# Pairwise products of fields: tile 0 of x in one transfer instead of four, and W issued after it

## The chip, the cores and the metric

The kernel runs on one core of one Trainium2 chip. The metric is the device time of one execution in microseconds (us). Before the change the median of four runs is 1289.72 us (1288.90 to 1290.04).

## The reference

`x` has 4096 samples of 32 fields with 64 values each, `W` is a 64 by 64 matrix, all in float32. Each field is multiplied by W, and then, for each of the 496 pairs of fields i < j, field i is multiplied element by element with the transformed field j.

```python
vid = jnp.einsum('bfd,de->bfe', x, W)
idx_i, idx_j = jnp.triu_indices(F_, k=1)
return x[:, idx_i, :] * vid[:, idx_j, :]
```

The output is 4096 x 496 x 64, some 520 MB, against 34 MB of input.

## The kernel before

**Tiles.** The batch is cut into 16 tiles of 256 samples. In a tile the 128 partitions hold 64 embedding values for each of two halves of the samples, and the free axis runs over 32 fields by 128 samples. A tile of x is thus 128 partitions by 4096 elements (2 MB), 16 KB in each partition. In HBM each partition's row of a tile has 8 fields of padding behind it.

**One large buffer.** `mem` (L122) holds everything in SBUF but W: places for tiles of x, given by `XPLACE`, and places for blocks of products, given by `SLOTS` as (number of pairs, place). The places overlap in time: a slot is written again after its transfer to HBM has ended. The first slots are 127 pairs at place 32, 126 pairs at place 159, and 63 pairs at place 32 again, so slot 2 needs the transfer of slot 0 to have ended.

**Work on a tile.** TensorE computes `vid` for a tile with 16 matmuls (L150): eight banks of four fields, two halves of the partitions each. In the profile each such matmul and its weight load count twice, so a tile has 32. `vid` fills all of PSUM and has one buffer, so the matmuls of the next tile wait for VectorE's reads of this one. VectorE writes the products into the slots with one `tensor_tensor` (L174) for each block that `by_block` and `products` lay out. The first block of a tile takes fields 0 to 15 alone, so VectorE's first product waits for the first half of the tile's matmuls. When a slot is full, SyncE issues its transfer to HBM (L177).

**Queues.** SyncE issues all transfers, in the order of the program, on one hardware queue served by 16 DMA engines. W goes first (L126), then tile 0 in four pieces of eight fields, then tiles 1 to 5 whole (all L135); 80 outputs (L177) and two further groups of five loads follow, the loads placed by `GROUPS`. A transfer that fills a place waits until what was there is no longer read.

The first matmul waits for W and for piece 1 of tile 0; the fifth, ninth and thirteenth wait for the other pieces.

Of the kernel before, what the change touches and what calls it, by code (L numbers as in the profile page):

```python
# [3 lines left out]

# [4 lines left out]

F32 = mybir.dt.float32  # L10
ALU = mybir.AluOpType

P = 128

C = 128

UNITS = 445

GROUPS = [6, 5, 5]
XPLACE = [285, 317, 349, 381, 413, 0, 285, 317, 349, 381, 413, 128, 96, 64, 32, 0]  # L20


SLOTS = [
    (127, 32), (126, 159), (63, 32), (64, 95), (84, 159), (63, 32),
    (74, 243), (84, 159), (95, 32), (71, 243), (116, 127), (95, 32),
    (106, 243), (116, 127), (95, 32), (106, 243), (116, 127), (95, 32),
    (127, 243), (116, 127), (95, 32), (127, 243), (116, 127), (43, 370),
    (95, 32), (95, 127), (63, 222), (95, 32), (84, 127), (74, 211),
    (84, 32), (95, 116), (74, 211), (116, 0), (95, 116), (74, 211),
    (116, 0), (95, 116), (105, 211), (105, 0), (105, 105), (105, 211),  # L30
    (105, 0), (105, 105), (127, 211), (105, 0), (105, 105), (127, 211),
    (105, 0), (106, 105), (56, 211), (95, 267), (51, 362), (107, 160),
    (73, 267), (73, 340), (84, 160), (84, 244), (95, 340), (84, 160),
    (95, 244), (105, 340), (84, 160), (96, 244), (105, 340), (105, 128),
    (106, 233), (105, 339), (127, 96), (116, 223), (106, 339), (127, 96),
    (116, 223), (106, 339), (127, 64), (127, 191), (127, 318), (127, 32),
    (127, 159), (120, 286),
]

XPAD = 8  # L40
OPAD = 24


STARTS = [0, *accumulate(n for n, _ in SLOTS)]


def by_block():


    def within(lo):  # L50
        yield "step", lo, 2, 1, 0
        for k in range(2):
            yield "step", lo, 4, 2, k
        for i in (lo, lo + 8):
            yield "row", i + 4, i, 4, 4
        yield "row", lo + 8, lo, 8, 8

    yield from within(0)
    yield "row", 16, 0, 16, 16
    yield from within(16)  # L60


def products(blocks, at=0):

    for kind, a, b, c, d in blocks:
        if kind == "row":
            rows, n, i0, di, j0, dj = c, d, b, 0, a, 1
        else:
            rows, n, i0, di, j0, dj = 16 // b, c, a, b, a + c + d, b
        r = k = 0  # L70
        while r < rows:
            room = STARTS[bisect_right(STARTS, at)] - at
            if k or room < n:
                m, w = 1, min(n - k, room)
            else:
                m, w = min(rows - r, room // n), n
            yield at, m, w, i0 + r * di + k, di, j0 + r * dj, dj
            at += m * w
            if k + w == n:
                r, k = r + m, 0  # L80
            else:
                k += w


def pairs(blocks):

    for _, m, w, i, di, j, dj in products(blocks):
        for r in range(m):
            for k in range(w):
                yield i + r * di + k, j + r * dj  # L90


@with_exitstack
def pairwise_bilinear_kernel(
    ctx: ExitStack,
    tc: tile.TileContext,
    x: bass.AP,
    w: bass.AP,
    out: bass.AP,
):  # L100

    nc = tc.nc
    NT = x.shape[0]
    F = x.shape[2] - XPAD
    D = P // 2
    NP = F * (F - 1) // 2

    BANK = 512 // C


    ctx.enter_context(tc.manual_schedule(engines={mybir.EngineType.SP}))

    const = ctx.enter_context(tc.tile_pool(name="const", bufs=1))
    psum = ctx.enter_context(
        tc.tile_pool(name="ps", bufs=1, space=bass.MemoryType.PSUM)
    )
    vid = psum.tile([P, F, C], F32)  # L120

    mem = const.tile([P, UNITS, C], F32)  # L122


    w2 = const.tile([P, D], F32)
    nc.sync.dma_start(out=w2, in_=w)  # L126

    loaded = []

    def load(pieces=1):  # L130
        t = len(loaded)
        xt = mem[:, XPLACE[t] : XPLACE[t] + F, :]
        n = F // pieces
        for lo in range(0, F, n):
            nc.sync.dma_start(out=xt[:, lo : lo + n, :], in_=x[t][:, lo : lo + n, :])  # L135
        loaded.append(xt)

    load(4)
    for _ in range(GROUPS[0] - 1):
        load()  # L140
    groups = iter(GROUPS[1:])

    for t in range(NT):
        xt = loaded[t]


        for b in range(0, F, BANK):
            for h in range(2):
                half = slice(h * D, (h + 1) * D)
                nc.tensor.matmul(  # L150
                    vid[half, b : b + BANK, :],
                    lhsT=w2[half, :],
                    rhs=xt[half, b : b + BANK, :],
                    start=True,
                    stop=True,
                )

        for at, m, w, i, di, j, dj in products(by_block(), t * NP):
            slot = bisect_right(STARTS, at) - 1
            n = m * w  # L160
            begin, end = STARTS[slot], STARTS[slot + 1]
            ot = mem[:, SLOTS[slot][1] : SLOTS[slot][1] + SLOTS[slot][0], :]
            o = ot[:, at - begin : at - begin + n, :]
            if m == 1:
                left = xt[:, i : i + w, :]
                right = vid[:, j : j + 1, :].to_broadcast([P, w, C])
            else:
                o = o.rearrange("p (m w) c -> p m w c", m=m)
                right = vid[:, j : j + (m - 1) * dj + 1 : dj, :].unsqueeze(2).to_broadcast([P, m, w, C])
                if di == 0:  # L170
                    left = xt[:, i : i + w, :].unsqueeze(1).to_broadcast([P, m, w, C])
                else:
                    left = xt.rearrange("p (m d) c -> p m d c", d=di)[:, i // di : i // di + m, i % di : i % di + w, :]
            nc.vector.tensor_tensor(o, left, right, ALU.mult)  # L174
            at += n
            if at == end:
                nc.sync.dma_start(out=out[:, begin:end, :], in_=ot)  # L177


        if t + 2 == len(loaded) < NT:  # L180
            for _ in range(next(groups)):
                load()


_INS = ["r_x", "L0_rec_W"]
_OUTS = [((4096, 496, 64), "float32")]


# [37 lines left out]
```

## Time and profile before

| | |
|---|---|
| median of 4 runs | 1289.72 us |
| the profiled execution, its time | 1289.47 us |
| its span, first to last instruction | 1287.7 us |
| VectorE busy | 1087.8 us, 407 instructions |
| TensorE busy, matmuls | 221.4 us, 512 records |
| moved by the DMA queue of SyncE | 553.69 MB |
| HBM read, written | 33.59 MB, 520.09 MB |

The page of the profile has busy times of each engine, the span in 40 slices, the DMA queues, the chain of work that ended last, and the costliest groups of instructions. The answers of the trace give instructions in order of time, the chain in a window, and busy times, DMA share and GB/s in any stretch. In a stretch's line the columns are: the stretch, its length, the busy times of TensorE's matmuls, its weight loads (PEld), VectorE (DVE) and GpSimd (POOL) with their counts, TensorE's granted clock, the share of the DMA engines, and the GB/s that started in it. A packet is booked at its start; in short stretches the share can so exceed 1. "SPq" is SyncE issuing a transfer.

### The profile page before, as it was taken

What the parts mean: (1) busy time and instruction counts of PE and PEld (TensorE: products, weight loads), DVE (VectorE), ACT (ScalarE), POOL (GpSimd) and SP (SyncE); (2) the same over time, 40 slices, a digit from 0 to 9 for tenths busy, and PEclk for the clock granted to TensorE, in tenths of its full rate; (3) what the DMA queues carried; (4) which work ended last, traced back from release to release, by engine and by line L of the source; (5) the groups of instructions that cost most, each with busy time, mean ns of one, the idle gap of its engine ahead of it and who ended that gap; (6) DMA issues with size and microseconds to landing.
All of it is one profiled execution on the core that took longest, in us unless ns stands there. A gap on an engine that the chain in (4) does not pass through costs nothing.

```text
span 1287.7 us, 1768 instructions
## 1 busy us (share of the span) xinstructions
PE 221.4 (17%) x512; PEld 41.0 (3%) x512; DVE 1087.8 (84%) x407; POOL 0.2 (0%) x4
## 2 busy tenths in 40 slices
PE   4031221312012013040313111103121121202000
PEld 1000000000000000000000000000000000000000
DVE  6799999998948399899999887369999998989960
POOL 0000000000000000000000000000000000000000
PEclk7555555556556555555555655555565565655555
DMA  9999999999999999999999999999999999999998
GB/s 386 455 414 443 426 430 448 433 436 432 424 435 415 427 435 428 441 431 436 428 443 434 427 438 423 429 428 436 430 437 437 432 433 437 433 435 433 430 442 359
DMA packets 14409, 553.79 MB, mean 430 GB/s; under 512 B 1728, under 2 KB 1728, under 8 KB 2240
## 3 DMA queue, kind: packets, MB, share of 16 engines
q1 hardware_dynamic: 14400, 553.69, 99.7%
q8 instruction: 4, 0.07, 0.0%
q14 instruction: 5, 0.04, 0.0%
HBM read 33.59 MB, written 520.09 MB: 430 GB/s over the span
## 4 chain that ended last, share of the span: by engine, by line
DMA 48%; DVE 45%; issue 3%; SPq 0%; PE 0%; another core or an unknown queue 0%; DVEq 0%
DMA out_dram<-mem 47%; DVE mem L174 45%; SPq L135 0%; PE vid L150 0%; DMA mem<-in_r_x_dram 0%; DVEq L214 0%; DVEq L174 0%; SPq L126 0%
## 5 line engine op out<-in xcount | busy, mean ns | idle before, releaser
L174 DVE TENSOR_TENSOR mem<-mem,vid 128x1024 f32<-128x1024 f32 (+16 forms) x407 | 1087.8, 2746 | 155.6 <-DMA out_dram<-mem 143.1
L150 PE MATMUL vid<-mem,w 64*64 64x512 f32 x512 | 221.4, 988 | 954.1 <-DVE mem L174 902.3
L150 PEld LDWEIGHTS vid<-mem,w 64*64 64x64 f32 x512 | 41.0, 196 | 1132.8 <-DVE mem L174 1061.5
L196 POOL MEMSET const-bfloat16-1.0<- 128x1 bf16 x1 | 0.1, 102 | 0.0
L196 POOL MEMSET const-uint8-127<- 128x1 uint8 x1 | 0.1, 102 | 0.0
L196 POOL MEMSET const-float32-0.0<- 128x1 f32 x1 | 0.1, 99 | 0.2 <-issue 0.2
L196 POOL MEMSET const-float32-1.0<- 128x1 f32 x1 | 0.1, 99 | 0.0
## 6 DMA issues: line engine op xcount, KB each, us to landing
out_dram<-mem SPq DMA_DIRECT2D x12, 8128.0 KB, 35.2
out_dram<-mem SPq DMA_DIRECT2D x13, 6720.0 KB, 32.9
out_dram<-mem SPq DMA_DIRECT2D x14, 6080.0 KB, 31.4
out_dram<-mem SPq DMA_DIRECT2D x9, 7424.0 KB, 31.6
out_dram<-mem SPq DMA_DIRECT2D x8, 5376.0 KB, 24.0
out_dram<-mem SPq DMA_DIRECT2D x6, 6784.0 KB, 34.7
mem<-in_r_x_dram SPq DMA_DIRECT2D x15, 2048.0 KB, 25.1
out_dram<-mem SPq DMA_DIRECT2D x4, 4736.0 KB, 26.7
```

The lines of the kernel that those rows point to most:

```text
L150: nc.tensor.matmul(vid[half, b : b + BANK, :], lhsT=w2[half, :], rhs=xt[half, b : b + BANK, :], start=True, stop=True,)
L174: nc.vector.tensor_tensor(o, left, right, ALU.mult)
L196: nc = _bacc.Bacc("TRN2", target_bir_lowering=False, num_devices=1, dynamic_dma_scratch_size=1024)
```

## The change

Tile 0 is loaded by one transfer of 128 x 4096 elements in place of four of 128 x 1024, and W's transfer (128 x 64) is issued after it. Tiles 1 to 5 follow W as before. The first matmul now waits for the whole of tile 0 and for W; no later matmul of tile 0 waits for a transfer. SyncE issues three transfers fewer. The order and shapes on TensorE and VectorE are as before.

```diff
     w2 = const.tile([P, D], F32)
-    nc.sync.dma_start(out=w2, in_=w)
 
     loaded = []
 
-    def load(pieces=1):
+    def load():
         t = len(loaded)
         xt = mem[:, XPLACE[t] : XPLACE[t] + F, :]
-        n = F // pieces
-        for lo in range(0, F, n):
-            nc.sync.dma_start(out=xt[:, lo : lo + n, :], in_=x[t][:, lo : lo + n, :])
+        nc.sync.dma_start(out=xt, in_=x[t][:, :F, :])
         loaded.append(xt)
 
-    load(4)
+    load()
+    nc.sync.dma_start(out=w2, in_=w)
     for _ in range(GROUPS[0] - 1):
         load()
```

## Prediction

> **What bounds the kernel now.** I read the 40 slices and the DMA queues of the page first, because a kernel that moves 554 MB is likely to be bound by that.
>
> ```profile
> DVE  6799999998948399899999887369999998989960
> ...
> DMA  9999999999999999999999999999999999999998
> ...
> q1 hardware_dynamic: 14400, 553.69, 99.7%
> ```
>
> The row to read is DMA: nine tenths or more in every slice, the first included. VectorE has slices of 3, 4 and 6 tenths, so it runs out of buffers and not out of time. One stretch from the view by stretches makes this sharper.
>
> ```profile
> 2.00:1283.00 1281.00, 221.38 (x512) 40.98 (x512) 1087.81 (x407) 0.00 (x0) 0.54 1.00 432
> ```
>
> The last two columns are the DMA share, 1.00, and GB/s, 432. From the first bytes to the last the 16 engines never stand still: time = first byte (about 2 us) + 553.69 MB at 432 GB/s + a tail. An edit can move the end only if it moves the first byte, changes what the bytes cost, or opens a hole in the stream. The list of waits agrees: VectorE's largest is 143.1 us in 34 waits for output transfers, so it is ahead of the stream and loses a delay at its next wait.
>
> The change lies in the first 35 us, so I next read the chain of waits there.
>
> ```profile
> 0.73 0.38 SPq L126
> 1.11 0.06 issue
> 1.17 4.05 DMA mem<-in_r_x_dram
> 5.21 0.14 issue
> 5.35 5.35 PE vid L150 x16
> 10.70 0.02 issue
> 10.73 34.48 DVE mem L174 x10
> ```
>
> W is issued at 0.73, piece 1 of tile 0 at 1.17, it lands at 5.21, TensorE starts 0.14 later and VectorE at 10.73. VectorE then runs through slots 0 and 1 without a gap. SyncE's timeline shows when slot 0 goes out, and the source view of that issue gives 24.8 us to landing:
>
> ```profile
> 28.23 0.35 SPq L177 DMA_DIRECT2D out_dram<-mem  x1
> ```
>
> **Is slot 0 late or early now?** The same two views give, for the last load (tile 5), issue at 5.46 and 28.4 us to landing: 33.86. Slot 0 lands at 28.23 + 24.8 = 53.03, which is 19.17 us after the loads; 8128 KB at 434 GB/s take just that. So slot 0 started only when the loads were through, and was issued about 5 us before its turn. The turn itself is in the narrow stretches:
>
> ```profile
> 32.00:32.50 0.50, 0.00 (x0) 0.00 (x0) 0.50 (x1) 0.00 (x0) 0.50 0.97 360
> 32.50:33.00 0.50, 0.00 (x0) 0.00 (x0) 0.50 (x1) 0.00 (x0) 0.50 2.42 1041
> ```
>
> A packet's bytes are booked at its start, and slot 0's packets (65 KB a partition) are the largest so far: the jump to 1041 GB/s is their start. The 16 engines turn to slot 0 between about 32.6 and 33.5; I call it 33.0. The cover from the issue at 28.23 is 4.8 us, from which the time between an issue and its first bytes has to be taken.
>
> **The change, part by part.**
>
> (a) *W no longer goes first.* Tile 0 is issued at 0.73 in W's place and not at 1.17: 0.44 us earlier. Bytes follow an issue by 1.0 us here: W, issued at 0.73, has its first in the stretch 1.70:1.80, and tile 0, issued at 1.17, its first in 2.20:2.30. Thus tile 0's bytes start near 1.8, and every load with them: -0.44 us for the stream.
>
> (b) *Four pieces become one transfer.* Three issues of about 0.43 us go from SyncE; SyncE is ahead of the stream anyway (the last load, issued at 5.46, lands at 33.86), so they are worth nothing. A partition's row becomes 16 KB in place of four of 4 KB. The pieces land 4.0, 4.9, 5.7 and 6.5 us after issues at 1.17, 1.64, 2.10 and 2.58, so at 5.2, 6.5, 7.8 and 9.1: about 1.29 us apart, 5.16 us for four. Whole tiles, landing at 13.95 (tile 1), 18.80, 23.73 and 28.65, are 4.9 us apart. Gain about 0.25 us; by rounding between 0.1 and 0.35.
>
> (c) *W sits behind tile 0.* Its 32 KB pass almost wholly between 1.70 and 2.10, before there is anything else to move. Now they stand in the full stream. The cost is between nothing and these 0.4 us; I take 0.2, since the bytes alone are below 0.1 us at 432 GB/s and the packets are small (256 B).
>
> The loads' end so moves by -0.44 - 0.25 + 0.2 = -0.5 us: slot 0's turn is 32.5 in place of 33.0.
>
> (d) *The first matmul waits for all of tile 0 and then W,* where it waited for a quarter of the tile. Tile 0 lands at 9.1 - 0.44 - 0.25 = 8.4, W 0.2 later at 8.6, and with the 0.14 us of before TensorE starts near 8.75 and not at 5.35: 3.4 us late. Queued behind that matmul on TensorE are the other 15 of tile 0; waiting for the first half of them is VectorE's first product, and for that SyncE's issue of slot 0.
>
> (e) *TensorE's first 5.35 us* set VectorE's start. Its weight loads show two paces:
>
> ```profile
> 7.08 0.27 PEld L150 LDWEIGHTS vid<-mem,w 64*64 64x64 f32 x2 [0.59 <-issue]
> 7.93 0.27 PEld L150 LDWEIGHTS vid<-mem,w 64*64 64x64 f32 x2 [0.59 <-issue]
> 8.79 0.16 PEld L150 LDWEIGHTS vid<-mem,w 64*64 64x64 f32 x2 [0.59 <-issue]
> 9.22 0.15 PEld L150 LDWEIGHTS vid<-mem,w 64*64 64x64 f32 x2 [0.28 <-issue]
> ```
>
> The steps are 0.86 us until 8.79, then 0.43, though the granted clock stands at 1.00 throughout. Piece 2 landed at 6.5 and is first needed at 7.93, so the pieces did not slow it. If the slow stretch goes with the start of work, it comes again and VectorE starts 3.4 us late, at 14.1. If it goes with the time since the program began, all eight steps are fast and 1.7 us come back; if nothing speeds up in time, four steps more are slow, +1.7. I take 3.4, the row as it stands. The Trainium skill ("TensorE: Matmul & The Clock Gate", section "What's actually happening") lets the clock rise after about 3.4 us of activity, in a window that runs freely: the 3.4 us from 5.35 to 8.79 agree, and by it the slow stretch returns with some scatter.
>
> (f) *Slot 0* is then issued at 28.23 + 3.4 = 31.6 in place of 28.23. Its bytes can start 1.0 us later by the rows in (a): 32.6. No row shows an output's own lead. The nearest hint is the stretch 30.50:31.00, the first in which the loads fall below 400 GB/s, 2.3 us after slot 0's issue: if that is its first effect, the bytes can start only at 33.9. Between 32.6 and 33.9 against a turn of 32.5 the hole is 0.1 to 1.4 us; I take 0.7.
>
> (g) *Behind slot 0* nothing is late. Slot 1 is issued 17.0 us behind slot 0 (45.22 now) and slot 0's transfer lasts 19.2 us. VectorE, which idles 7.94 us until slot 0's buffer is free, idles less instead. The hole passes on as it is; there is no spare time in a stream with a share of 1.00 to win it back.
>
> **Sum.** -0.5 (a to c) + 0.7 (f) = +0.2 us. The profiled execution took 1289.47 us, 1.8 more than its span of 1287.7, and that remainder is untouched. It lies 0.25 below the median of 1289.72, so as a median I say 1289.9. A difference of 0.2% (2.6 us) is about what a measurement of this kernel can tell from no change.
>
> A rule that speaks against the change: the Trainium skill, "Perfetto Trace Analysis", section "DMA Optimizations", says that splitting a transfer can let some of the work start sooner, if the DMA engines are generally idle. Here 3.4 us of TensorE's start go with the split, but the DMA share is 1.00, so the rule's condition fails. By the rule alone the end would be 3.4 us later; by the rows above, 0.2.
>
> **Rivals.**
>
> *A, the cover suffices.* The slow stretch of TensorE does not come again, or an output's lead is under 0.9 us. There is no hole, the stream keeps the gain of (a) to (c), and the time is 1289.7 - 0.5 = 1289.2. For it: slot 0's cover of 4.8 us. Against it: 3.4 + 1.0 use 4.4 of it, and the turn comes 0.5 sooner.
>
> *B, W is late and a hole opens: slower.* Its place is W's transfer, issued between tile 0 and tile 1. If its small packets do not pass in order but share the engines with tile 1, W lands with tile 1, near 13.95 - 0.5 = 13.4; TensorE starts at 13.6, 8.2 us late, slot 0 is issued at 36.4 and flows at 37.4, 4.9 us behind its turn: +4.4 us with the gain taken off, 1294.1. The change turns slower by over 2.6 us when slot 0 is issued after about 34.6 (32.5 + 0.5 + 2.6 - 1.0), that is when TensorE starts after 11.7. Against it: loads land strictly in the order of issue in this trace.
>
> *C, a longer cold start.* Slow steps all along (+1.7) and the long lead (2.3) add up: slot 0 flows at 28.23 + 5.1 + 2.3 = 35.6, 3.1 behind its turn, +2.6: 1292.3. It needs both at once.
>
> *D, the edit changes nothing.* The four pieces are one block in memory and in HBM, so they could have flowed as one all along. But the landings 1.29 us apart and TensorE's start at the first show that they count one by one.
>
> **How the numbers follow.** Forecast, a small hole about cancelled by the gain: 0.62, 1289.3 to 1291.0. A: 0.26, 1288.6 to 1289.4. C, whole or in part: 0.08. B: 0.04. The forecast, A but for 0.01 of it, and half of C lie within 0.2%: same 0.91. Slower 0.08 from B and the rest of C. Faster gets A's 0.01: nothing in (a) to (c) is worth 2.6 us. The range, 1288.7 to 1291.6, takes in the forecast, nearly all of A and the lower half of C.
>
> **What would show it.** In the profile after: tile 0's single landing near 8.4 and W's near 8.6; TensorE from 8.75; VectorE from 14.1; slot 0 issued at 31.6; a short hole or none near 32.5 to 33.5 in the narrow stretches; slot 0's landing within 1 us of 53.03. I would be wrong if W landed well past 9, if the DMA share fell anywhere later, or if VectorE's lateness were still to be seen after slot 2.

## The result, and the profile after

The changed kernel takes 1291.04 us (median of 42 runs, 1289.48 to 1292.11), the kernel before 1289.57 us (60 runs, 1288.81 to 1291.02). The ratio is 1.0011 with a 95% interval of 1.0007 to 1.0015: slower by 1.5 us. That lies within the forecast range of 1288.7 to 1291.6 and within 0.2%, but the likeliest case said +0.2 us, and the median lies just above the 1289.3 to 1291.0 that the forecast gave that case. So the question for the experiments is where the other 1.3 us come from. The profiled execution has a span of 1289.0 us where before had 1287.7.

The 40 slices and the long stretch of the changed kernel show almost nothing; this is what a change of 0.1% looks like in an average.

```profile
DMA  9999999999999999999999999999999999999998
...
2.00:1284.00 1282.00, 220.88 (x512) 41.11 (x512) 1087.91 (x407) 0.00 (x0) 0.55 1.00 432
```

The chain of waits of the changed kernel in the first 75 us answers to the one of before:

```profile
0.73 0.37 SPq L132
1.10 0.05 issue
1.15 7.75 DMA w<-in_L_rec_W_dram
8.90 0.14 issue
9.03 5.84 PE vid L148 x16
14.88 0.02 issue
14.90 34.48 DVE mem L172 x10
49.38 0.02 issue
49.40 22.70 DMA out_dram<-mem
```

W is now what TensorE waits for; it lands at 8.90. TensorE starts 3.7 us later than before, needs 5.84 us for the first half of tile 0 and not 5.35, and VectorE starts 4.2 us later. VectorE's 34.48 us are the same to the hundredth. Slot 0 is issued 17.5 us after VectorE's start, at 32.40:

```profile
32.40 0.35 SPq L175 DMA_DIRECT2D out_dram<-mem  x1
```

The narrow stretches of the changed kernel show the hole (DMA share and GB/s are the last two columns):

```profile
31.00:31.50 0.50, 0.07 (x2) 0.07 (x4) 0.50 (x2) 0.00 (x0) 0.50 1.15 492
31.50:32.00 0.50, 0.50 (x2) 0.22 (x4) 0.50 (x1) 0.00 (x0) 0.50 0.39 164
32.00:32.50 0.50, 0.50 (x4) 0.16 (x2) 0.50 (x2) 0.00 (x0) 0.50 0.08 33
32.50:33.00 0.50, 0.50 (x4) 0.07 (x2) 0.50 (x1) 0.00 (x0) 0.50 0.00 0
33.00:33.50 0.50, 0.50 (x4) 0.23 (x2) 0.50 (x1) 0.00 (x0) 0.50 4.88 2081
```

Before, there was no stretch without bytes between the loads and slot 0. Now the loads are through near 32, nothing starts between 32.5 and 33.0, and then all 16 engines begin their 65 KB packets within one half microsecond: 2081 GB/s is twice the 1041 and 1040 of the two stretches of before, since there the engines came to slot 0 one after another. The packet records of the trace give the same in finer steps. The first packets of slot 0 start between 32.72 and 33.53 us before, and between 33.25 and 33.40 after. The hole has set the engines **in step**.

### The profile page after: what moved, and what is told of

Same layout as the page of the kernel before. It is cut to its first block, busy times and chain, and to the rows that moved or that the text cites. A ratio compares the mean times of both kernels' runs of the same rounds, so it can differ in the third digit from the quotient of the medians.

```text
span 1289.0 us, 1764 instructions
## 1 busy us (share of the span) xinstructions
PE 220.9 (17%) x512; PEld 41.1 (3%) x512; DVE 1087.9 (84%) x407; POOL 0.2 (0%) x4
## 4 chain that ended last, share of the span: by engine, by line
DMA 51%; DVE 42%; issue 2%; SPq 0%; PE 0%; another core or an unknown queue 0%; DVEq 0%
DMA out_dram<-mem 50%; DVE mem L172 42%; DMA w<-in_L_rec_W_dram 1%; SPq L132 0%; PE vid L148 0%; DVEq L212 0%; DVEq L172 0%
```

## The experiments

Theory H: the cost is the hole before slot 0, and the hole comes from slot 0's readiness alone. Its rival R: the single transfer, or W's small packets in the full stream, cost in themselves. In the table, "flow" is the start of slot 0's first packets (of its first part where it is cut in two); "landing" is the end of the last packets of the whole of slot 0, averaged over the 16 engines (the prediction's 53.03 is the moment at which the last engine reported it, which is later); the medians have the kernel before on the same chip beside them.

| run | flow, us | landing, us | median, us | before, us | ratio (95% interval) |
|---|---|---|---|---|---|
| before | 32.7 to 33.5 | 52.21 | 1289.57 | | |
| the change | 33.25 to 33.40 | 52.57 | 1291.04 | 1289.57 | 1.0011 (1.0007 to 1.0015) |
| e1 whole tile, W first | 33.24 to 33.39 | 52.56 | 1291.28 | 1289.61 | 1.0012 (1.0004 to 1.0021) |
| e2 pieces, W second | 32.4 to 33.7 | 52.17 | 1289.29 | 1289.61 | 0.9999 (0.9990 to 1.0008) |
| e3 change, slot 0 in two | no hole | 52.25 | 1289.04 | 1289.61 | 0.9995 (0.9986 to 1.0004) |
| e4 W after tile 1 | 37.22 to 37.37 | 56.54 | 1295.86 | 1289.61 | 1.0047 (1.0034 to 1.0060) |
| e6 before, slot 0 in two | no hole | 52.36 | 1289.89 | 1289.33 | 1.0004 (0.9995 to 1.0013) |
| e7 pieces, W last | 33.70 to 33.85 | 53.02 | 1291.12 | 1289.33 | 1.0014 (1.0006 to 1.0023) |

**e1, the whole tile with W first.**

```diff
-    load(4)
+    load(1)
```

> One part of the change alone: tile 0 in one transfer, W still first. Theory H (the time is set by when slot 0 can flow; after the loads the stream stands still until then): tile 0 lands near 9.0, TensorE starts near 9.2, slot 0 is issued near 32.5 as in the changed kernel, so the hole is about as large and the time is 1290.8 to 1291.3, as with the whole change. Rival R (the cost is W's small packets inside the full stream, or W landing last): W lands at 2.5 again, so the time falls back to 1289.3 to 1289.7.

It took 1291.28 us, as H said: W is in place long before, and the time is that of the whole change.

**e2, four pieces with W behind the first.**

```diff
             nc.sync.dma_start(out=xt[:, lo : lo + n, :], in_=x[t][:, lo : lo + n, :])
+            if t == 0 and lo == 0:
+                nc.sync.dma_start(out=w2, in_=w)
```

(and W's first issue taken out)

> The gain of an early tile 0 without its cost: four pieces, W behind piece 1. H: piece 1 lands near 4.8 and W near 5.0, TensorE starts near 5.2, slot 0 is issued near 28.2, no hole; the stream starts 0.4 us earlier, so 1289.1 to 1289.6, at or just under the kernel before. R (W's packets in the full stream cost): 1290 or more.

1289.29 us. TensorE starts at 4.63, slot 0 is issued at 27.79, and there is no hole. W's small packets stand in the full stream here and do no harm; R falls on both its halves together with e1 and e7.

**e3, the changed kernel with slot 0 in two transfers.**

```diff
-    (127, 32), (126, 159), (63, 32),
+    (56, 32), (71, 88), (126, 159), (63, 32),
```

> The changed kernel with slot 0 cut in two transfers, 56 and 71 pairs, at the same places; no VectorE instruction changes. The first is ready near 23 us, well before the loads end. H: the hole is gone although TensorE still starts near 9.0, and the time falls to 1288.9 to 1289.6. R (the single transfer, or W's place in the stream, costs in itself): stays at 1291.0.

1289.04 us, 2.0 us under the changed kernel. The chain of this run shows that nothing was mended in front:

```profile
1.16 7.72 DMA w<-in_L_rec_W_dram
8.88 0.14 issue
9.01 6.06 PE vid L148 x16
15.07 0.02 issue
15.09 28.26 DVE mem L172 x9
```

TensorE and VectorE start as late as in the changed kernel. But the first part of slot 0 is issued at 23.00, the loads run into it without a gap, and the late start costs nothing. Against the kernel before the median is 0.57 us lower; the interval takes in no change.

**e6, the same cut in the kernel before.** The edit is that of e3.

> Control for the run with slot 0 in two: the same cut in the kernel before, where slot 0 is not late. H: nothing to win, 1289.3 to 1289.8. If the cut itself brought the gain: 1288.8 or less.

1289.89 us, just above the upper end: the cut itself wins nothing, and e3's gain is the hole's.

**e7, four pieces with W behind all of them.**

```diff
-    nc.sync.dma_start(out=w2, in_=w)
...
     load(4)
+    nc.sync.dma_start(out=w2, in_=w)
```

> The other part alone: tile 0 in four pieces, W behind all four. H: W lands near 9.0, TensorE starts near 9.1, slot 0 flows near 33.3 as in the changed kernel: a hole of the same kind and 1290.8 to 1291.4. R (the single transfer is what costs): 1289.3 to 1289.7.

1291.12 us. Either part of the change alone brings the whole cost (1.7 us in e1 and 1.8 in e7 over the kernel before, 1.5 for both together), and the two do not add up, since each only sets when TensorE has both W and data.

**e4, more of it: W behind tile 1 as well.**

```diff
     load()
+    load()
     nc.sync.dma_start(out=w2, in_=w)
-    for _ in range(GROUPS[0] - 1):
+    for _ in range(GROUPS[0] - 2):
```

> Dose: the changed kernel with W behind tile 1 as well, so W lands near 13.7, TensorE starts near 13.9 and slot 0 is issued near 37.2, 4.9 us later than in the changed kernel. H: the hole grows by as much and passes on one for one: 1295.4 to 1296.2. If VectorE's lead won some of it back, or the hole were not the cause, less: 1291 to 1293.

1295.86 us. In the narrow stretches the hole is plain; between 32.5 and 37.0 the engines stand still.

```profile
34.00:36.00 2.00, 0.60 (x2) 0.29 (x4) 2.00 (x2) 0.00 (x0) 0.50 0.00 0
36.00:37.00 1.00, 1.00 (x4) 0.23 (x2) 1.00 (x2) 0.00 (x0) 0.50 0.00 0
37.00:37.50 0.50, 0.50 (x4) 0.23 (x2) 0.50 (x1) 0.00 (x0) 0.50 4.87 2081
```

Slot 0 flows 3.97 us later than in the changed kernel, and the span of the profiled execution is 4.1 us longer (1293.1 against 1289.0). More hole passes on one for one between these two executions; e4's is the fastest of its five, and the medians are 4.8 us apart. The 4.9 us expected of slot 0's issue were 4.0, because TensorE's first half took 5.00 us in this execution.

**What is still open after these.** In the changed kernel slot 0 lands 0.36 us later than before (52.57 against 52.21), and the end is 1.5 us later. Something is lost behind slot 0. The stretches at work show where. First before, then the changed kernel:

```profile
54.00:140.00 86.00, 15.77 (x32) 2.33 (x32) 83.20 (x35) 0.00 (x0) 0.50 1.00 433
170.00:340.00 170.00, 31.40 (x72) 5.71 (x72) 160.11 (x56) 0.00 (x0) 0.55 1.00 434
```

```profile
54.00:140.00 86.00, 15.53 (x32) 2.33 (x32) 83.02 (x35) 0.00 (x0) 0.52 1.00 431
170.00:340.00 170.00, 30.93 (x72) 5.71 (x72) 159.25 (x56) 0.00 (x0) 0.56 1.00 433
```

The DMA share is 1.00 in all four, so no engine idles, yet the bytes move more slowly. In the packet records, bytes over duration give the rate of one engine while it works (large packets alone, so e5's own small writes are left out):

| GB/s per engine | 54 to 113 us | 170 to 340 us | 840 to 1280 us |
|---|---|---|---|
| before, e2, e3, e6 | 27.05 | 27.08 | 27.08 |
| the change, e1, e4, e7 | 26.94 | 27.02 | 27.08 |
| e5 (six writes) | 27.02 | 27.02 | 27.08 |
| e11 (one write) | 26.98 | 27.02 | 27.08 |

The two upper rows agree to 0.01 in every one of their kernels, so this is no scatter: kernels with a hole move their packets 0.4% and then 0.2% more slowly, until about the second group of loads, and not at all after it. From slot 0's landing to that of the output near 341 us the stream takes 288.22 us before and 289.15 after, averaged over the engines: 0.93 us. Theory L: engines that the hole has put in step slow one another. Rivals: the output rows' places in HBM collide when the engines are in step (P), or something else is late.

**e8, e9 and e10, other row distances in HBM** (the kernel changed, changed, and before).

```diff
-OPAD = 24
+OPAD = 26   # e8, e10
+OPAD = 32   # e9
```

> The changed kernel with the padding behind each output row in HBM at 26 units of 512 B in place of 24, so that rows of neighbouring partitions lie at other distances. If the packets between 54 and 340 us are slow behind the hole because engines in step write to rows that collide in HBM (theory P), their rate there moves away from 26.94 and 27.02 GB/s per engine, up or down by 0.1 or more. If it is the engines being in step as such (theory L), the rates stay within 0.02 of these, and the time near 1291.

> The same with 32 units. P: another rate again, by 0.1 or more off 26.94 and 27.02. L: both stay within 0.02, time near 1291.

> Control: the kernel before with 26 units, where the engines are spread over 0.8 us from the start. L: 27.05 and 27.08 GB/s per engine as before, 1289.3 to 1289.9. P: its rate moves too, by 0.05 or more.

e8 took 1290.96 us (ratio to before 1.0014, 1.0005 to 1.0024) with 26.94 and 27.02 GB/s per engine; e9 took 1290.85 (1.0014, 1.0004 to 1.0023) with 26.94 and 27.02; e10 took 1289.31 (1.0002, 0.9992 to 1.0011) with 27.05 and 27.08. No rate moves with these two distances: P falls for them.

**e5 and e11, the engines put out of step again.** Small writes right behind slot 0 keep some engines longer than others.

```diff
                 nc.sync.dma_start(out=out[:, begin:end, :], in_=ot)
+                if slot == 0:   # e5
+                    for p0, p1, u in (0, 14, 0), (0, 11, 7), (0, 9, 14), (16, 23, 0), (16, 21, 7), (16, 18, 14):
+                        nc.sync.dma_start(out=out[p0:p1, NT * NP + u : NT * NP + u + 7, :], in_=ot[p0:p1, u : u + 7, :])
...
+                if slot == 0:   # e11
+                    nc.sync.dma_start(out=out[0:8, NT * NP : NT * NP + 24, :], in_=ot[0:8, 0:24, :])
```

> The changed kernel with six small writes issued right behind slot 0, into the unused rows behind the output: 3.5 KB from each of 14, 11, 9, 7, 5 and 2 partitions, so that the DMA engines, which the hole has set to the same phase, are spread over about 0.8 us again. They cost 0.4 us averaged over the engines and 0.8 for the one hit most; the output is the reference's. Theory L (engines in step move packets more slowly): from slot 0's landing to the landing of the output issued before the second group of loads the stream takes 288.2 to 288.5 us averaged over the engines, as without a hole, in place of 289.15, and the packets between 54 and 113 us move at 27.04 GB/s per engine in place of 26.94; the time is 1290.4 to 1291.3, no worse than the changed kernel. Rival (the loss behind slot 0 comes from late fetches or waits, not from the engines' phase): 289.1 and 26.94 stay, and the writes come on top: 1291.4 to 1291.9.

> The changed kernel with one write right behind slot 0, 12 KB from each of 8 partitions into the unused rows behind the output, so that 8 of the 16 DMA engines fall about 0.46 us behind the other 8 (0.23 us averaged); the output is the reference's. Theory L (engines in step slow one another, whichever they are): with only 8 in step the loss is about halved, 26.99 GB/s per engine or more between 54 and 113 us and 27.05 between 170 and 340, and the time stays at 1290.7 to 1291.2. If the slowing is between engines that this write shifts together: 26.94 and 27.02 stay, and the write comes on top, 1291.2 to 1291.6. If it is between engines that it parts: 27.05 and 27.08 return, 1290.3 to 1290.7.

Both are misses in time: e5 took 1293.87 us (ratio to before 1.0031, 1.0020 to 1.0042), e11 1292.18 (1.0018, 1.0009 to 1.0027). The writes cost far more than I gave them: e11's 12 KB packets took 1.6 to 2.2 us each, where 0.46 was expected. The stretch from slot 0's landing to the output near 341 us, for which e5's expectation had 288.2 to 288.5 us under L and 289.1 under its rival, took 290.1; the writes' own cost is in it, so it decides nothing. In the packets right behind, L does show. Slot 1's 128 packets of 64,512 bytes last 2.380 us in all cases before, in 16 after the change (the others up to 2.41), in 101 in e5 and in 57 in e11. Parting the engines so brings back the flat duration, for a time. It does not last: between 170 and 340 us e5 and e11 are at 27.02 like the changed kernel, where L had 27.05 or more.

The starts of the packets say more. Near 298 us, in the changed kernel, 14 of the 16 engines still start within 0.22 us of one another. In e5 at the same place the 16 starts are spread over 2.08 us of a packet's 2.40, wider than the 1.74 of before, and the packets are as slow as the changed kernel's. So being in step cannot be the whole cause there. L is supported right behind slot 0, where the phase was set by hand; what slows the packets between 170 and 340 us stays open.

## Why the prediction was right, and where it was not

**(a) to (c), the gain of 0.5 us.** Right. Tile 0's first packet starts at 1.74 in place of 2.21. The times are too coarse for the three terms, but the landings, as the engines report them and averaged over the 16, tell them apart. The last piece of tile 0 landed at 8.56 before and at 8.10 in e7, where the pieces go first: 0.46 us for (a), forecast 0.44. Tile 0 in one transfer landed at 8.30 in e1, where W goes first as before: 0.26 for (b), forecast 0.25. Tile 1 followed tile 0 by 5.00 us in the changed kernel and 5.01 in e7, with W between them, and by 4.90 in e1 and 4.89 before: 0.1 for (c), forecast 0.2. That makes 0.6 us. The whole sum without a hole is e3: 0.57 us under before, though its interval takes in zero.

**(d) TensorE's start.** 9.03, forecast 8.75. Tile 0 landed at 8.7 and not 8.4: on average over the engines it landed at 7.8, but one of the 16 was half a microsecond behind the others, and TensorE waits for the last.

**(e) TensorE's two paces.** The slow steps came again, as taken, and five of them in place of four: 5.84 us. The first half's weight loads show the turn near 13.5:

```profile
11.62 0.26 PEld L148 LDWEIGHTS vid<-mem,w 64*64 64x64 f32 x2 [0.59 <-issue]
12.47 0.26 PEld L148 LDWEIGHTS vid<-mem,w 64*64 64x64 f32 x2 [0.59 <-issue]
13.33 0.22 PEld L148 LDWEIGHTS vid<-mem,w 64*64 64x64 f32 x2 [0.59 <-issue]
13.83 0.15 PEld L148 LDWEIGHTS vid<-mem,w 64*64 64x64 f32 x2 [0.28 <-issue]
14.26 0.15 PEld L148 LDWEIGHTS vid<-mem,w 64*64 64x64 f32 x2 [0.28 <-issue]
```

The granted clock of 1.00 that the prediction set against the slow steps was no reading: the stretches print 1.00 wherever the trace has no clock record. The first record begins at 8.8 us before and at 13.5 after, and in all 13 profiles it begins where the pace changes. Over the profiles of this case the first half of tile 0 took from 5.00 (e4) to 6.61 us (e5) with nothing changed in it. The Trainium skill ("TensorE: Matmul & The Clock Gate", section "What's actually happening") says that the number of slow matmuls varies from run to run, because the window that sets the clock runs freely. The rows agree, and scatter widely around the 3.4 us of before: from TensorE's first matmul to the change of pace it is 2.7 (e8) to 6.0 us (e5). Where there is a hole this variation should reach the end, since no cover hides it. In the five profiles with a hole of about this size the shortest span goes with VectorE's earliest start (e8, 14.43: 1288.3 us) and the longest with its latest (e7, 15.36: 1290.2). That it is also why the changed kernel spreads over 2.6 us in its 42 runs is not shown: e2 spreads over 2.1 us in 11 without a hole.

**(f) The hole.** Mechanism right, size at the upper end. The lead from issue to bytes was 0.85 us, less than both of my ends. The hint for the long lead was misread: 30.50:31.00 is not the first stretch under 400 GB/s, since 10.50:11.00 has 360, long before slot 0's issue. But the issue came at 32.40 and not 31.6, and the loads ended, averaged over the engines, at 31.94 and not 33.04, 0.6 us of it already at tile 4 (27.05 against 27.66) and 0.5 in tile 5, which slot 0 no longer slows. The hole was 1.4 us where I took 0.7. Slot 0 flows 0.3 us later than before, where I had 0.2: the errors cancel, and up to here the sum holds.

**(g) The step that failed:** "The hole passes on as it is." Slot 0 landed 0.36 us late on average, the output near 341 us 1.3 us, the last one 1.75 us. By the engine that lands last, it is 0.01 (53.04 against 53.03), 1.3 and 1.5 us. VectorE's lateness is gone by slot 2, issued at 61.84 in both kernels, as forecast; the loss is in the stream. The term that I had at nothing is worth 1.1 to 1.5 us. Of it 0.93 us are the slower packets between slot 0 and 341 us, shown in every kernel with a hole and in none without. Another 0.3 to 0.5 us come between 341 and 440 us, around the second group of loads; the profiles of kernels with a hole need 98.0 to 98.2 us for that part and those without 97.6 to 97.8. What takes them stays open. That the result still lies in the range is partly luck: this term alone is several times the +0.2 us of the sum, and the upper part of the range, where the median fell, had been set for C's longer cold start. I had read the share of 1.00 as "nothing can be lost", but a share of busy time says only that the engines work, not at what rate.

**The rivals.** A (no hole) is what e3 and e2 make by hand, at the time it gave: 1289.2 against 1289.04 and 1289.29. B did not come: W landed at 8.90, right behind tile 0. C's two conditions did not come together, but half of one did (one more slow step). By the Trainium skill's rule on splitting ("Perfetto Trace Analysis", section "DMA Optimizations") I had estimated 3.4 us; the rows gave 0.2, the chip 1.5. The rule's condition, engines generally idle, is not met over the span, but e1, which leaves out the split alone and takes 1.7 us more than the kernel before, shows that the split does count here, at the one place where the engines run dry.

## What to carry to other kernels

On a stream that is always full, a late start of the computing costs nothing as long as the first output is issued before the loads end; count the cover from issue to turn, less the lead of about 1 us, and mind that TensorE's first matmuls vary by more than 1 us from run to run. If the cover is short, cutting the first output (e3) mends it as well as cutting the first load. A hole can cost more than its length, so price it from a run and not from the gap.

## What the runs showed of the hardware that I had not expected

- Behind a start of 65 KB packets within 0.15 us of one another (54 to 113 us) the DMA engines moved 26.94 GB/s each; behind a start spread over 0.8 us they moved 27.05, with every packet of slot 1 at 2.380 us. Later (170 to 340 us) a spread of 2.1 us in e5 did not bring the higher rate back.
- Packets of 12 KB from 8 partitions, written next to a full stream, took 1.6 to 2.2 us each, near the 2.38 us of the 64,512-byte packets beside them.
- With an output queued behind the loads the last load takes longer: from tile 4's landing to tile 5's, averaged over the engines, 5.4 us before the change, 5.0 in e2 and about 6 in e3, and 4.9 in all of the change, e1, e4 and e7, where the output came after the loads.
- TensorE's steps fell from 0.85 to 0.43 us 2.7 to 6.0 us after its first matmul, over 13 profiles of the same 16 matmuls, and the trace's first clock record begins there. Ahead of it the profile prints a granted clock of 1.00, which is the absence of a record.
